# An LSTM cell in another order: a scan over pairs for the cell state, and the product of two transposed halves for the output

## The chip, the cores and the metric

One core of a Trainium2 chip. The metric is the device time of one execution in microseconds (us). Before the change: 1159.02 us, the median of three runs (1155.53 to 1159.16).

Engines are called as in the profile: PE (matrix engine; PEld is its weight load), DVE (vector), ACT (scalar), POOL (GpSimd), SP (it issues DMAs here). A name with a q at its end, such as DVEq, is the engine's sequencer.

## The reference

A graph network of two layers over 1250 nodes with 512 features, then an LSTM over the 1250 rows in order, both with a residual sum. The change touches the LSTM only. With x_t a row and h, c the state (512 values each):

```
f_t = sigmoid([x_t, h] W_f + b_f)      i_t = sigmoid([x_t, h] W_i + b_i)
g_t = tanh([x_t, h] W_c + b_c)         o_t = sigmoid([x_t, h] W_o + b_o)
c_t = f_t * c + i_t * g_t
h_t = o_t * tanh(c_t)
```

The output is x_t + h_t. All data are fp32.

## The kernel before, in words

The graph network and the part of the gates that depends on x alone (the products with the upper halves of the weights) take the first 557 us. Their sums are written to HBM (xp_d) as three bf16 planes for each row. The rest is the recurrence, in `lstm` (from line 759).

**Stretches.** The 1250 rows are cut into 32 stretches (P) of 40 rows (LEN), which run side by side. Each stretch starts from a zero state 90 rows early (WARM), so `lstm` runs 130 steps: 90 to warm up, 40 that give output. At the end the states at the ends of the stretches are compared with those that the next stretches had at their start (lines 813 to 824); only if they are apart would `in_order` run all rows one after the other. It did not run in the profiled execution.

**Layout.** On 128 partitions lie 4 blocks of 128 hidden values times 32 stretches. The state is cut once more along its free dimension into two halves s of 64 values. A tile of gates `p` is 128 x 4 x 64 in PSUM: forget, input, output, candidate.

**A step** (lines 796 to 808). `open_step` loads xs by SP and opens the gate sums with a small bf16 matmul (L532). `add_gates` (L540) adds h times the recurrent weights: 32 matmuls, which the profile counts as 64 instructions, since each has two in fp32. Their order is written by hand: 12 matmuls that need only half 0 of h, then 8 that close the gates of half 0 and need half 1 of h, then 12 more, which close the gates of half 1.

**The cell** (L547 to L558) runs once for each half: tanh of the candidate into the second half of tile cg, sigmoid of f and i, sigmoid of o; one product of (f, i) with (c, g), one sum into the first half of cg, tanh of it, the product with o, and a transpose in blocks of 32 x 32 on DVE into hT, which is what PE takes as weights in the next step.

**What sets the order.** The block stands under `tc.manual_schedule` for PE, DVE and ACT: these engines work through their instructions in the order of the program text, half 0's cell ahead of half 1's. Waits between engines, and of an engine for its own results, are put in by the framework as semaphores. hT has two buffers, the tiles of pool lstm_work (cells) three. In the 40 steps with output POOL adds hh to the residual x2c (L806), and after steps 8, 16, 24, 32, 38 and 40 the rows are stored by DMA.

Of the kernel before, what the change touches and what calls it, by code (L numbers as in the profile page):

```python
# [9 lines left out]
F32 = mybir.dt.float32  # L10
# [3 lines left out]
AF = mybir.ActivationFunctionType  # L14
OP = mybir.AluOpType
# [23 lines left out]
def gnn_lstm_kernel(  # L39
# [23 lines left out]
    nc = tc.nc  # L63
# [122 lines left out]
    with ExitStack() as gnn_stack:  # L186
# [14 lines left out]
        with tc.tile_pool(name="prep", bufs=1) as prep, \  # L201
# [20 lines left out]
            for name, v in (("fcb", fc_b), ("b1", b_1), ("b2", b_2)):  # L222
                b = prep.tile([R, D], F32, name=name)
# [317 lines left out]
                                     Wh[:, b, j, :, 64 * s:64 * (s + 1)],  # L541
                                     start=False, stop=(b == 3))

        def cell(pool, p, cg, s, hh, hT):

            m = slice(64 * s, 64 * (s + 1))
            nc.scalar.activation(cg[:, 1, :], p[:, 3, :], AF.Tanh)  # L547
            sg = pool.tile([128, 2, 64], F32, name=f"sg{s}")
            nc.scalar.activation(sg, p[:, 0:2, :], AF.Sigmoid)  # L549
            so = pool.tile([128, 64], F32, name=f"so{s}")  # L550
            nc.scalar.activation(so, p[:, 2, :], AF.Sigmoid)  # L551
            pr = pool.tile([128, 2, 64], F32, name=f"pr{s}")
            nc.vector.tensor_mul(pr, sg, cg)  # L553
            nc.vector.tensor_add(cg[:, 0, :], pr[:, 0, :], pr[:, 1, :])  # L554
            th = pool.tile([128, 64], F32, name=f"th{s}")
            nc.scalar.activation(th, cg[:, 0, :], AF.Tanh)  # L556
            nc.vector.tensor_mul(hh[:, m], so, th)  # L557
            nc.vector.transpose(hT.rearrange("p b c -> p (b c)"), hh[:, m])  # L558

        def in_order(pool, ps_g, Wh):  # L560

            cgs = [pool.tile([128, 2, 64], F32, name=f"cgs{s}") for s in range(2)]
            hT0 = [pool.tile([128, 2, 32], F32, name=f"hTs{s}") for s in range(2)]
            for s in range(2):
                nc.vector.memset(cgs[s], 0.0)
                nc.vector.memset(hT0[s], 0.0)
            with tc.For_i(0, N, 1) as t:
                xs = pool.tile([128, G], F32, name="xs")
                xr = pool.tile([128, 128], F32, name="xr")
                for j in range(4):  # L570
                    nc.sync.dma_start(
                        xs[32 * j:32 * (j + 1), :],
                        bass.AP(tensor=xw_d.tensor, offset=xw_d.offset + t * (4 * G) + j * G,
                                ap=[[0, 32], [1, G]]))
                    nc.sync.dma_start(
                        xr[32 * j:32 * (j + 1), :],
                        bass.AP(tensor=x2_d.tensor, offset=x2_d.offset + t * D + 128 * j,
                                ap=[[0, 32], [1, 128]]))
                x4 = xs.rearrange("p (g m) -> p g m", g=NG)
                ps = open_gates(ps_g, lambda j: ident[:, 32 * j:32 * (j + 1)],  # L580
                                lambda j, s: x4[:, :, 64 * s:64 * (s + 1)])
                add_gates(ps, hT0, Wh)
                hh = pool.tile([128, 128], F32, name="hhs")
                h1 = [pool.tile([128, 2, 32], F32, name=f"hT1{s}") for s in range(2)]
                for s in range(2):
                    cell(pool, ps[s], cgs[s], s, hh, h1[s])
                    nc.vector.tensor_copy(hT0[s], h1[s])
                nc.vector.tensor_add(xr, xr, hh)
                for j in range(4):
                    nc.sync.dma_start(  # L590
                        bass.AP(tensor=out.tensor, offset=out.offset + t * D + 128 * j,
                                ap=[[D, 1], [1, 128]]),
                        xr[32 * j:32 * j + 1, :])
# [165 lines left out]
        def lstm(late, Wh):  # L759

            TOL = 2.0 ** -18
            with tc.tile_pool(name="state", bufs=2) as state, \
                    tc.tile_pool(name="load", bufs=5) as load, \
                    tc.tile_pool(name="lstm_work", bufs=3) as cells, \
                    tc.tile_pool(name="seq", bufs=1) as seq, \
                    tc.tile_pool(name="ps_g", bufs=3, space=PSUM) as ps_g, \  # L770
                    tc.tile_pool(name="ps_c", bufs=1, space=PSUM) as ps_c:
                cgs = [seq.tile([128, 2, 64], F32, name=f"cg{s}") for s in range(2)]

                def keep_state(dst, hT):
                    for s in range(2):
                        nc.vector.tensor_copy(dst[:, 2 * s:2 * s + 2, :], hT[s])
                        nc.vector.transpose(
                            dst[:, 4 + 2 * s:6 + 2 * s, :].rearrange("p b c -> p (b c)"),
                            cgs[s][:, 0, :])

                x2c = base1.rearrange("b t (q m) -> b t q m", q=4)
                for j in range(4):
                    for i in range(T):
                        (nc.sync if i % 2 else nc.gpsimd).dma_start(
                            x2c[32 * j:32 * (j + 1), i, :, :], x2[:, i, 128 * j:128 * (j + 1)])
                x2c = x2c.rearrange("b i q m -> b (i q) m")
                snap = seq.tile([128, 8, 32], F32, name="snap")
                last = seq.tile([128, 8, 32], F32, name="last")
                stores = [8, 16, 24, 32, 38, LEN]
                with tc.manual_schedule(engines={mybir.EngineType.PE, mybir.EngineType.DVE,  # L790
                                                 mybir.EngineType.Activation}):
                    hT = [state.tile([128, 2, 32], F32, name=f"hT{s}") for s in range(2)]
                    for s in range(2):
                        nc.vector.memset(cgs[s], 0.0)
                        nc.vector.memset(hT[s], 0.0)
                    for n in range(-WARM, LEN):
                        if n == 0:
                            keep_state(snap, hT)
                        ps = open_step(load, ps_g, n)
                        add_gates(ps, hT, Wh)  # L800
                        hh = cells.tile([128, 128], F32, name="hh")
                        hT = [state.tile([128, 2, 32], F32, name=f"hT{s}") for s in range(2)]
                        for s in range(2):
                            cell(cells, ps[s], cgs[s], s, hh, hT[s])
                        if n >= 0:
                            nc.gpsimd.tensor_add(x2c[:, n, :], x2c[:, n, :], hh)  # L806
                            if n + 1 in stores:
                                store(x2c, ([0] + stores)[stores.index(n + 1)], n + 1)
                    keep_state(last, hT)

                apart = seq.tile([128, 8, 31], F32, name="apart")
                nc.vector.tensor_sub(apart, last[:, :, 0:31], snap[:, :, 1:32])
                nc.vector.scalar_tensor_tensor(apart, apart, -1.0, apart, op0=OP.mult, op1=OP.max)
                nc.vector.tensor_scalar(apart, apart, TOL, None, OP.is_le)
                near = seq.tile([128, 1], F32, name="near")
                nc.vector.tensor_reduce(near, apart.rearrange("p a b -> p (a b)"),
                                        mybir.AxisListType.X, OP.add)
                pc = ps_c.tile([1, 1], F32, name="pc")  # L820
                nc.tensor.matmul(pc, near, ones, start=True, stop=True)
                far = seq.tile([1, 1], I32, name="far")
                nc.vector.tensor_scalar(far, pc, -1.0, float(128 * 8 * 31), OP.mult, OP.add)
                n_far = nc.values_load(far, min_val=0, max_val=128 * 8 * 31)
                with tc.If(n_far > 0):
                    for i in range(T):
                        pl = pl_bufs[:, i % 2, :, :]
                        nc.sync.dma_start(pl.rearrange("b i g -> b (i g)"), tile_steps(i))
                        v = h.rearrange("b t d -> b (t d)")[:, :4 * G]
                        nc.vector.tensor_add(v, pl[:, 0, :], pl[:, 1, :])  # L830
                        nc.vector.tensor_add(v, v, pl[:, 2, :])
                        nc.sync.dma_start(in_time(xw_d, i), v)
                        nc.gpsimd.dma_start(in_time(x2_d, i), x2[:, i, :])
                    in_order(seq, ps_g, Wh)
# [57 lines left out]
```

## Time and profile before

| What | Value |
|---|---|
| Time of the profiled execution | 1157.69 us |
| Its span (first to last instruction) | 1155.9 us |
| Mean granted PE clock | 0.989 (1.00 from 557 to 1150 us) |
| Busy: PE, PEld, DVE, ACT, POOL | 1025.9, 535.2, 519.3, 344.4, 69.8 us |
| From 557 to 1150 us: PE, DVE, ACT, POOL busy | 511.3, 244.9, 202.7, 18.4 us |
| ACT: cg L547, sg L549, so L551, th L556, each x260 | 224, 271, 230, 256 ns |
| DVE: pr L553, cg L554, hh L557, hT L558, each x260 | 272, 225, 225, 246 ns |
| POOL: sum L806, x40 | 461 ns |

How to read it: a group of the page is a line of the source, an engine, the operation, its result and its sources, the shapes, how many there were, then the busy time in us and the mean of one in ns, and last the idle time of the engine just before them with what ended it. In the chain of waits, "issue" is time that no instruction fills. Matmuls are pipelined and their ends are modelled, so a busy PE is not a PE at its peak.

### The profile page before, as it was taken

The page shows a single profiled execution, that of the slowest core. Times are in us where ns is not written, and L with a number is a line of the kernel's source. Part 1 is how long each engine was busy: PE and PEld are TensorE (multiplying, and loading weights), DVE is VectorE, ACT ScalarE, POOL GpSimd, SP SyncE. Part 2 cuts the span into 40 slices and gives each one's busy share as a digit, 9 for nine tenths or more (in the row PEclk, how much of TensorE's full clock was granted, in tenths as well). Part 3 has the DMA queues.
Part 4 walks back from the last instruction along what each step waited for, and adds up shares of the span by engine and source line. Part 5 has one row for each costly group of instructions (what it writes and reads, how often), then busy time and mean ns, then how long its engine had stood idle before and what let it go on. Part 6 is the DMA issues. An engine that isn't in the chain of part 4 may idle for free.

```text
span 1155.9 us, 27516 instructions
## 1 busy us (share of the span) xinstructions
PE 1025.9 (89%) x11340; PEld 535.2 (46%) x11356; DVE 519.3 (45%) x1775; ACT 344.4 (30%) x1284; POOL 69.8 (6%) x123
## 2 busy tenths in 40 slices
PE   2999997799999999999788888888888888888886
PEld 1555544355455444444344444444444444444443
DVE  4956665401500665555444444444434444443444
ACT  2312212412500023333333333333333333333332
POOL 1000000300000281000000000000000000010011
PEclk9999999799999999999999999999999999999999
DMA  8000000800300175222632323232322333333331
GB/s 233 1 1 1 1 1 2 256 1 1 89 1 1 69 168 181 109 110 109 199 97 84 97 84 98 84 98 84 94 87 87 95 88 94 102 97 102 102 102 21
DMA packets 41466, 96.22 MB, mean 83 GB/s; under 512 B 6125, under 2 KB 21846, under 8 KB 39928
## 3 DMA queue, kind: packets, MB, share of 16 engines
q1 hardware_dynamic: 35012, 77.59, 22.3%
q0 software_dynamic: 4496, 14.09, 4.2%
q10 hardware_dynamic: 1819, 2.65, 0.8%
q8 instruction: 92, 1.51, 0.6%
q14 instruction: 47, 0.38, 0.1%
HBM read 71.93 MB, written 19.76 MB: 79 GB/s over the span
## 4 chain that ended last, share of the span: by engine, by line
PE 67%; DVE 16%; ACT 9%; issue 4%; DMA 3%; POOL 0%; DVEq 0%; ACTq 0%; SPq 0%
PE gates L540 28%; PE psM L166 15%; PE agg L685 11%; PE psM L510 10%; DVE pr L553 3%; ACT th L556 3%; DVE hT L558 3%; DVE hh L557 3%; DVE cg L554 3%; ACT cg L547 3%; PE acc L303 2%; ACT sg L549 2%; DMA base<-in_x_dram 2%; DMA bx<-in_L_ffn_b_i_dram 1%; PE psT L155 1%
## 5 line engine op out<-in xcount | busy, mean ns | idle before, releaser
L540 PE MATMUL gates<-Wh,hT 128*32 128x256 f32 x8320 | 482.5, 383 | 75.2 <-DVE hT L558 75.2
L540 PEld LDWEIGHTS gates<-Wh,hT 128*32 128x32 f32 x8320 | 244.7, 110 | 287.1 <-DVE hT L558 151.9
L553 DVE TENSOR_TENSOR pr<-sg,cg 128x128 f32<-128x128 f32 x260 | 70.6, 272 | 223.9 <-ACT sg L549 223.8
L685 PE MATMUL agg<-adj,planes 128*128 128x512 bf16 (+1 forms) x704 | 134.6, 352 | 10.0 <-ACT planes L415 7.2
L510 PE MATMUL psM<-Wx,xT 128*128 128x512 f32 x320 | 138.7, 594 | 1.5 <-ACT xT L160 1.5
L547 ACT ACTIVATE cg<-gates 128x64 f32<-128x64 f32 x260 | 58.2, 224 | 249.2 <-PE gates L540 245.6
L556 ACT ACTIVATE th<-cg 128x64 f32<-128x64 f32 x260 | 66.7, 256 | 138.6 <-DVE cg L554 138.6
L685 PEld LDWEIGHTS <-planes 128*128 128x128 bf16 x720 | 71.8, 100 | 73.0 <-ACT planes L415 7.6
L557 DVE TENSOR_TENSOR hh<-so,th 128x64 f32<-128x64 f32 x260 | 58.6, 225 | 86.4 <-ACT th L556 86.0
L510 PEld LDWEIGHTS psM<-Wx,xT 128*128 128x128 f32 x320 | 60.4, 190 | 76.8 <-issue 72.9
L558 DVE STREAM_TRANSPOSE hT<-hh 128x64 f32<-128x64 f32 x260 | 63.8, 246 | 27.9 <-DVE hh L557 0.9
L166 PE MATMUL psM<-w,hT 128*128 128x512 f32 x160 | 70.9, 596 | 0.0
L549 ACT ACTIVATE sg<-gates 128x128 f32<-128x128 f32 x260 | 70.5, 271 | 0.2
L554 DVE TENSOR_TENSOR cg<-pr 128x64 f32<-128x64 f32 x260 | 58.5, 225 | 8.9
L806 POOL TENSOR_TENSOR base<-base,hh 128x128 f32<-128x128 f32 x40 | 18.4, 461 | 693.0 <-issue 533.4
L551 ACT ACTIVATE so<-gates 128x64 f32<-128x64 f32 x260 | 59.8, 230 | 0.0
L532 PE MATMUL gates<-xs,sel 96*32 96x256 bf16 x1040 | 52.5, 272 | 4.2 <-DMA xs<-xp_d 4.2
L303 PE MATMUL acc<-od,ob 125*128 125x400 f16 (+22 forms) x360 | 47.9, 260 | 9.0 <-DVE od L289 8.2
L289 DVE TENSOR_SCALAR od<-ids,key 125x820 f16<-125x820 f16 (+42 forms) x160 | 55.6, 347 | 0.0
L287 DVE TENSOR_SCALAR ob<-ids,low 125x128 f16<-125x128 f16 x160 | 39.5, 247 | 16.3 <-PE acc L303 16.0
L166 PEld LDWEIGHTS psM<-w,hT 128*128 128x128 f32 x160 | 29.7, 190 | 34.0 <-issue 33.0
L303 PEld LDWEIGHTS <-ob 125*128 125x128 f16 x360 | 29.7, 98 | 31.6 <-issue 12.7
(154 smaller groups left out, 663.6 us busy)
## 6 DMA issues: line engine op xcount, KB each, us to landing
xs<-xp_d SPq DMA_DIRECT2D x130, 384.0 KB, 3.2
xp_d<-planes SPq DMA_DIRECT2D x10, 1536.0 KB, 5.4
w<-in_L_gnn_w_dram POOLq DMA_DIRECT2D x4, 1024.0 KB, 12.8
xp_d<-adj POOLq DMA_DIRECT2D x1, 1440.0 KB, 7.8
base<-x SPq DMA_DIRECT2D x20, 64.0 KB, 2.3
base<-x POOLq DMA_DIRECT2D x20, 64.0 KB, 2.6
fcw<-in_L_gnn_fc_w_dram POOLq DMA_DIRECT2D x1, 1024.0 KB, 8.6
out_dram<-base SPq DMA_DIRECT2D x12, 64.0 KB, 2.2
```

The source lines that it names most:

```text
L166: nc.tensor.matmul(p, lT[:, k, :], rhs[:, k, :], start=(k == 0), stop=(k == KD - 1))
L303: nc.tensor.matmul(blocks[i][:, (d0 - i * BW) * T:(d1 - i * BW) * T], ob, od[:, (d0 - lo) * T:(d1 - lo) * T], start=False, stop=last)
L510: nc.tensor.matmul(p, yT[:, k, :], Wx[:, k, j, :, :], start=(k == 0), stop=(k == KD - 1))
L540: nc.tensor.matmul(ps[s][32 * j:32 * (j + 1), :, :], hT[b // 2][:, b % 2, :], Wh[:, b, j, :, 64 * s:64 * (s + 1)], start=False, stop=(b == 3))
L547: nc.scalar.activation(cg[:, 1, :], p[:, 3, :], AF.Tanh)
L549: nc.scalar.activation(sg, p[:, 0:2, :], AF.Sigmoid)
L553: nc.vector.tensor_mul(pr, sg, cg)
L554: nc.vector.tensor_add(cg[:, 0, :], pr[:, 0, :], pr[:, 1, :])
L556: nc.scalar.activation(th, cg[:, 0, :], AF.Tanh)
L557: nc.vector.tensor_mul(hh[:, m], so, th)
L558: nc.vector.transpose(hT.rearrange("p b c -> p (b c)"), hh[:, m])
L685: nc.tensor.matmul(p[:, :n * R], planes[:, k, pl, f * 128:(f + 1) * 128], adj[:, k, t0:t0 + n, :].rearrange("b i r -> b (i r)"), start=(k ...
```

## The change

`cell` is replaced by a class `Half`, one object for each half, with tiles that live through all steps. `fi` is a tile of pairs (0, sigmoid value), `add` a tile of pairs (g, f*c), `c` the result of a scan over these pairs. Along the free dimension the scan computes state = data0 * state + data1. With data0 = (0, i) and data1 = (g, f*c) each pair yields first g and then i*g + f*c, which is the new cell state, at the second place of the pair. So there are 128 elements in the scan for 64 values of the state. Output gate and tanh of the cell are then transposed each by itself, and their product is written to hT at once. h without a transpose is no longer made on DVE: POOL computes it in the 40 steps with output.

```diff
-        def cell(pool, p, cg, s, hh, hT):
-
-            m = slice(64 * s, 64 * (s + 1))
-            nc.scalar.activation(cg[:, 1, :], p[:, 3, :], AF.Tanh)
-            sg = pool.tile([128, 2, 64], F32, name=f"sg{s}")
-            nc.scalar.activation(sg, p[:, 0:2, :], AF.Sigmoid)
-            so = pool.tile([128, 64], F32, name=f"so{s}")
-            nc.scalar.activation(so, p[:, 2, :], AF.Sigmoid)
-            pr = pool.tile([128, 2, 64], F32, name=f"pr{s}")
-            nc.vector.tensor_mul(pr, sg, cg)
-            nc.vector.tensor_add(cg[:, 0, :], pr[:, 0, :], pr[:, 1, :])
-            th = pool.tile([128, 64], F32, name=f"th{s}")
-            nc.scalar.activation(th, cg[:, 0, :], AF.Tanh)
-            nc.vector.tensor_mul(hh[:, m], so, th)
-            nc.vector.transpose(hT.rearrange("p b c -> p (b c)"), hh[:, m])
+        class Half:
+            def __init__(self, pool, s):
+                self.s = s
+                self.fi = [pool.tile([128, 2, 64, 2], F32, name=f"fi{s}{n}") for n in range(2)]
+                self.add = [pool.tile([128, 64, 2], F32, name=f"ad{s}{n}") for n in range(2)]
+                self.c = pool.tile([128, 64, 2], F32, name=f"c{s}")
+                self.n = 0
+                for t in self.fi:
+                    nc.vector.memset(t, 0.0)
+            def begin(self):
+                nc.vector.memset(self.c, 0.0)
+            def step(self, pool, p, so, tc, hT):
+                m = slice(64 * self.s, 64 * (self.s + 1))
+                fi, add = self.fi[self.n], self.add[self.n]
+                self.n = 1 - self.n
+                nc.scalar.activation(fi[:, :, :, 1], p[:, 0:2, :], AF.Sigmoid)
+                nc.scalar.activation(add[:, :, 0], p[:, 3, :], AF.Tanh)
+                nc.scalar.activation(so[:, m], p[:, 2, :], AF.Sigmoid)
+                nc.vector.tensor_mul(add[:, :, 1], fi[:, 0, :, 1], self.c[:, :, 1])
+                nc.vector.tensor_tensor_scan(
+                    *(t.rearrange("p m a -> p (m a)") for t in (self.c, fi[:, 1, :, :], add)),
+                    0.0, OP.mult, OP.add)
+                soT = pool.tile([128, 64], F32, name=f"soT{self.s}")
+                nc.vector.transpose(soT, so[:, m])
+                nc.scalar.activation(tc[:, m], self.c[:, :, 1], AF.Tanh)
+                tcT = pool.tile([128, 64], F32, name=f"tcT{self.s}")
+                nc.vector.transpose(tcT, tc[:, m])
+                nc.vector.tensor_mul(hT.rearrange("p b c -> p (b c)"), soT, tcT)
...
-                        hh = cells.tile([128, 128], F32, name="hh")
+                        so = cells.tile([128, 128], F32, name="so")
+                        th = cells.tile([128, 128], F32, name="th")
                         hT = [state.tile([128, 2, 32], F32, name=f"hT{s}") for s in range(2)]
                         for s in range(2):
-                            cell(cells, ps[s], cgs[s], s, hh, hT[s])
+                            halves[s].step(cells, ps[s], so, th, hT[s])
                         if n >= 0:
-                            nc.gpsimd.tensor_add(x2c[:, n, :], x2c[:, n, :], hh)
+                            nc.gpsimd.tensor_mul(th, so, th)
+                            nc.gpsimd.tensor_add(x2c[:, n, :], x2c[:, n, :], th)
```

`in_order` and `keep_state` are changed to the new names in the same way; the two clears of cg become clears of `c`, and four clears of the `fi` tiles come before the loop.

More of the change, by code (lines that the diff above doesn't have):

```diff
@@ L560, in in_order @@
         def in_order(pool, ps_g, Wh):
-            cgs = [pool.tile([128, 2, 64], F32, name=f"cgs{s}") for s in range(2)]
+            halves = [Half(pool, s) for s in range(2)]
             hT0 = [pool.tile([128, 2, 32], F32, name=f"hTs{s}") for s in range(2)]
             for s in range(2):
-                nc.vector.memset(cgs[s], 0.0)
+                halves[s].begin()
                 nc.vector.memset(hT0[s], 0.0)
@@ L582, in in_order @@
                 add_gates(ps, hT0, Wh)
-                hh = pool.tile([128, 128], F32, name="hhs")
-                h1 = [pool.tile([128, 2, 32], F32, name=f"hT1{s}") for s in range(2)]
+                so = pool.tile([128, 128], F32, name="sos")
+                th = pool.tile([128, 128], F32, name="ths")
                 for s in range(2):
-                    cell(pool, ps[s], cgs[s], s, hh, h1[s])
-                    nc.vector.tensor_copy(hT0[s], h1[s])
-                nc.vector.tensor_add(xr, xr, hh)
+                    h1 = pool.tile([128, 2, 32], F32, name=f"hT1{s}")
+                    halves[s].step(pool, ps[s], so, th, h1)
+                    nc.vector.tensor_copy(hT0[s], h1)
+                nc.vector.tensor_mul(so, so, th)
+                nc.vector.tensor_add(xr, xr, so)
                 for j in range(4):
@@ L771, in lstm @@
                     tc.tile_pool(name="ps_c", bufs=1, space=PSUM) as ps_c:
-                cgs = [seq.tile([128, 2, 64], F32, name=f"cg{s}") for s in range(2)]
+                halves = [Half(seq, s) for s in range(2)]
                 def keep_state(dst, hT):
@@ L778, in keep_state @@
                             dst[:, 4 + 2 * s:6 + 2 * s, :].rearrange("p b c -> p (b c)"),
-                            cgs[s][:, 0, :])
+                            halves[s].c[:, :, 1])
                 x2c = base1.rearrange("b t (q m) -> b t q m", q=4)
@@ L793, in lstm @@
                     for s in range(2):
-                        nc.vector.memset(cgs[s], 0.0)
+                        halves[s].begin()
                         nc.vector.memset(hT[s], 0.0)
```

## The prediction

> **What bounds the kernel now.** I read the page first: busy shares, the chain that ended last, the groups. PE is busy 89% of the span, yet the groups show that its recurrent matmuls wait for a transpose on the Vector engine.
>
> ```profile
> PE 67%; DVE 16%; ACT 9%; issue 4%; DMA 3%; POOL 0%; DVEq 0%; ACTq 0%; SPq 0%
> ...
> L540 PE MATMUL gates<-Wh,hT 128*32 128x256 f32 x8320 | 482.5, 383 | 75.2 <-DVE hT L558 75.2
> ```
>
> The LSTM fills the stretch from 557 to 1150 us, so 130 steps hold about half of the span, and the change lies in this half alone. So I next read the chain of waits over one step (start, duration, what).
>
> ```profile
> 803.02 0.22 ACT cg L547
> 803.25 0.18 ACT sg L549
> ...
> 803.45 0.30 DVE pr L553
> 803.75 0.02 issue
> 803.77 0.24 DVE cg L554
> ...
> 804.03 0.27 ACT th L556
> ...
> 804.32 0.24 DVE hh L557
> 804.56 0.03 issue
> 804.59 0.02 DVEq L558
> 804.61 0.04 issue
> 804.65 0.26 DVE hT L558
> ```
>
> This is half 0. Every piece is end to end: the next matmul starts at 804.96, 1.93 us after the first activation. Note the two kinds of gap on DVE. Between pr and cg it is 0.02; ahead of hT, which waits for hh on its own engine and for PE (which still reads the older hT buffer), a sequencer piece DVEq appears and the gap is 0.09. By the timeline's durations the gaps are 0.034 and 0.107. In the last 37 steps hh of half 0 waits for ACT and for POOL, and its gap grows from 0.03 to 0.10: a second engine to wait for costs 0.07 when the wait that comes last sits in the sequencer.
>
> Then I asked the timeline whether half 1 has slack.
>
> ```profile
> 804.65 0.25 DVE L558 STREAM_TRANSPOSE hT<-hh 128x64 f32<-128x64 f32 x1
> 804.82 0.25 DVE L553 TENSOR_TENSOR pr<-sg,cg 128x128 f32<-128x128 f32 x1
> 804.95 1.02 PEld L540 LDWEIGHTS gates<-Wh,hT 128*32 128x32 f32 x24 [0.83 <-DVE hT L558]
> 805.11 0.23 DVE L554 TENSOR_TENSOR cg<-pr 128x64 f32<-128x64 f32 x1
> 805.37 0.26 ACT L556 ACTIVATE th<-cg 128x64 f32<-128x64 f32 x1 [0.54 <-DVE cg L554]
> 805.99 0.24 DVE L558 STREAM_TRANSPOSE hT<-hh 128x64 f32<-128x64 f32 x1
> 806.28 1.89 PEld L540 LDWEIGHTS gates<-Wh,hT 128*32 128x32 f32 x40 [0.31 <-DVE hT L558]
> ```
>
> PE has 24 instructions that need only half 0. Sixty-four take 3.70 us with a tail of 0.40, so four start every 0.22 us and six fours last 1.32. Half 1's weights start 806.28 - 804.95 = 1.33 after half 0's. So half 1 is just in time, with no slack: its work on DVE begins only when half 0's hT is through. A step is therefore 1.33 (half 0's start to half 1's start) + 1.20 (16 more PE instructions, to the first activation) + 1.93 (half 0's cell) = 4.46 us. Both cells are on the path: a delay in half 0's counts, and a delay of half 1's behind it counts again.
>
> [...] No run here shows a scan yet. [...] 224 ns for 64 elements at L554, 291 (median of L553) for 128. [...] the set of sigmoid holds tanh too, and a load takes some 1283 ns. The trace agrees: 1.28 us, twice, and none after the first Sigmoid although Tanh follows 259 times. [...] I price the strided operands at nothing. No run here shows one[...].
>
> **The change, half 0.** Times count from the first activation. Old: pr at 0.42, cg ends at 0.98, th 1.01 to 1.27, hh from 1.30, hT ends at 1.88, PE at 1.93.
> - Sigmoid of f and i goes first (271 ns). The product f*c waits only for it: starts at 0.30, where pr starts at 0.42 (a gain of 0.12), and takes 0.224 for 64 elements, to 0.53. Tanh of the candidate starts 0.16 later than the sigmoid by ACT's spacing and ends by 0.39: covered by that product.
> - The scan needs the product (its own engine) and the candidate (ACT), of which DVE has not yet waited for the latter. That is a wait on two engines. In this trace the sequencer's separate wait was for DVE whenever an instruction waited for DVE and another engine (hT: DVE there, PE with the instruction), so the late wait sits there and the gap is 0.107; the other end is 0.034. I take 0.107. Start 0.63.
> - The scan itself: [...] I take 0.424: ends at 1.06, where cg ended at 0.98.
> - Tanh of the cell 1.09 to 1.35. The transpose of the output gate (0.246) lies on DVE meanwhile, done by 1.31 even if it starts 0.01 after the scan: hidden by tanh. If tanh did not cover it, 0.25 per half.
> - Transpose of tanh from 1.38 to 1.63, then the product. It writes hT, so the wait for PE moves from the transpose to it, with the same 0.107: 1.73 to 1.96, PE at 2.01. From tanh's end to PE is 0.66, as before: the two operations change places for nothing.
> Half 0 costs 2.01 - 1.93 = 0.08 a step.
>
> **Half 1.** DVE is in order: half 0's final product stands ahead. From the end of half 0's last DVE operation: the first product starts 0.08 early, as pr does, and ends at 0.11; scan 0.21 to 0.64 (cg ended at 0.43); tanh to 0.93; transpose 0.96 to 1.21; product 1.31 to 1.54; PE 0.05 later at 1.59, where it was 1.38. So PE waits 0.20 a step longer. The gain of 0.12 from the earlier sigmoid does not exist here, since the gates are ready long before DVE is.
>
> **Sum.** 0.08 + 0.20 = 0.285 us by unrounded terms; times 130 steps 37.0 us.
> - Table load: the load before L549 is on the chain (the first step takes 5.77 instead of 4.46). With Sigmoid first, its set is loaded while ACT waits for PE: -1.3 us.
> - Four clears of 128 x 256 (0.27 each, from 0.11 and 0.17 for 64 and 128): they lie before the first scan, while PE still waits for the first xs, and the first recurrent matmul waits only for the small clears, from 557.5 to 558.0, against its start at 561.3. Zero; without the cover 1.1 us.
> - hh's wait for POOL (0.07 in the last 37 steps) passes to tanh of the cell: no difference.
> - POOL gets a product beside the sum, 2 x 0.46 us in steps of 4.5: hidden. No DMA is issued or moved. After the last step POOL starts earlier by some 0.26 and works 0.5 longer, while DVE's comparison and the read of its result run to the end: zero.
> Against the profiled execution (1157.69, span 1155.9): 1157.69 + 37.0 - 1.3 = **1193.4 us**. That run lies 1.3 below the median shown, within its spread.
>
> **Rivals.**
> - **Faster**: the scan with the gap before it costs what the add it replaces does: 0.291 + 0.034 = 0.325. For it speaks that the old add sits 0.034 behind pr[...]. Then half 0 gains 0.123 and half 1 keeps its 1.33: -0.125 x 130 - 1.3, **1140 us**. The point that decides: gap and scan together below 0.39 make the kernel faster; I expect 0.531.
> - **Scan at one element a cycle, but behind the slow gap** (0.398 together): +0.02 a step, **1159 us**, no change.
> - **Half throughput, the gap the short one**: 0.146 a step less than forecast, **1174.5 us**.
> - **The product f*c waits for the candidate's tanh too**, because the two write alternate elements of one tile: it starts at 0.41, the scan then waits for one engine: 0.25 a step, **1189 us**.
> - **Three cycles an element, or strides that cost as much**: 0.133 in each half on top, **1228 us**.
>
> **How the numbers follow.** Chances: forecast 0.52, short gap 0.14, candidate waited for 0.08, three cycles 0.07 (all slower, 0.81); one element a cycle behind the slow gap 0.07 (same); faster 0.12. About 0.3%, 3.5 us, is what a measurement can tell from no change. The range reaches from the unchanged case up to the forecast with hundredths for the strides: 1157 to 1203 leaves out the faster case and the three cycles, 0.19.
>
> **What would show it.** In the changed profile: a scan group x260 of 0.42 us; a DVEq piece ahead of the scan and of the last product, none ahead of the transposes; the first product 0.30 after the sigmoid; half 1's 40 weight loads about 1.54 after half 0's 24, with idle time on PE waiting for half 1's hT; no table load inside the first step. A scan of 0.29 or a gap of 0.03 ahead of it makes the prediction wrong by the sizes above; so does a step shorter than 4.46 us.

## The result, and the profile after

The changed kernel takes 1211.7 us (median of six runs, 1210.2 to 1214.0), the kernel before 1159.4 beside it: ratio 1.046, interval 1.044 to 1.048. The profiled execution took 1210.81 us with a span of 1209.0. The forecast was 1193.4 with a range up to 1203: slower as expected, but by 52 us instead of 36.

The page's shares and groups after the change:

```profile
PE 50%; DVE 29%; ACT 11%; issue 6%; DMA 3%; DVEq 1%; ACTq 1%; POOL 0%
...
L540 PE MATMUL gates<-Wh,hT 128*32 128x256 f32 x8320 | 505.2, 383 | 106.7 <-DVE hT L578 100.5
...
L566 ACT ACTIVATE fi<-gates 128x128 f32<-128x128 f32 x260 | 74.3, 286 | 257.2 <-PE gates L540 257.1
...
L570 DVE TENSOR_TENSOR_SCAN c<-fi,ad 128x128 f32<-128x128 f32 x260 | 110.5, 425 | 27.2 <-DVE ad L569 0.5
...
L578 DVE TENSOR_TENSOR hT<-soT,tcT 128x64 f32<-128x64 f32 x260 | 69.6, 268 | 27.6 <-DVE tcT L577 0.9
```

DVE's share of the chain rose from 16 to 29%, PE's fell from 67 to 50%. The scan takes 425 ns, as priced (0.424 us). One row is odd: a product of 64 elements into hT takes 268 ns on the mean, where L554 and L557 took 225.

The chain of waits over half 0 of one warm-up step:

```profile
804.90 0.30 ACT fi L566
805.20 0.02 issue
805.22 0.24 DVE ad L569
805.46 0.03 issue
805.49 0.02 DVEq L570
805.51 0.04 issue
805.55 0.43 DVE c L570
805.99 0.02 issue
806.01 0.27 ACT th L575
...
806.30 0.26 DVE tcT L577
...
806.65 0.22 DVE hT L578
806.88 0.15 DVE ad L569
```

The chain goes from half 0's hT straight on into half 1's first product on DVE. Before, it went from hT to PE. The sequencer piece stands ahead of the scan, with a gap of 0.09. From the first activation to the end of hT it is 1.98 us. The timeline of the same step shows what PE gets:

```profile
806.79 0.22 DVE L569 TENSOR_TENSOR ad<-fi,c 128x64 f32<-128x64 f32 x1
806.93 1.02 PEld L540 LDWEIGHTS gates<-Wh,hT 128*32 128x32 f32 x24 [0.93 <-DVE hT L578]
807.12 0.42 DVE L570 TENSOR_TENSOR_SCAN c<-fi,ad 128x128 f32<-128x128 f32 x1
...
808.22 0.22 DVE L578 TENSOR_TENSOR hT<-soT,tcT 128x64 f32<-128x64 f32 x1
808.50 1.88 PEld L540 LDWEIGHTS gates<-Wh,hT 128*32 128x32 f32 x40 [0.55 <-DVE hT L578]
```

Half 1's weights start 1.57 us after half 0's (808.50 - 806.93), against 1.33 before, and PE's weight loads sit idle for the difference (0.55 us ahead of half 1's, 0.31 before). A warm-up step is 4.80 us (median; 4.46 before), close to the 4.745 forecast. But a step with output is 5.15, where it was 4.53 before: 0.27 more than the 0.34 that the warm-up steps lost. The timeline of one such step, at half 1's end:

```profile
1103.46 0.24 DVE L577 STREAM_TRANSPOSE tcT<-th 128x64 f32<-128x64 f32 x1 [0.20 <-ACT th L575]
1103.78 0.45 POOL L829 TENSOR_TENSOR th<-so,th 128x128 f32<-128x128 f32 x1 [4.16 <-DVE tcT L577]
1103.81 0.51 DVE L578 TENSOR_TENSOR hT<-soT,tcT 128x64 f32<-128x64 f32 x1
...
1104.37 1.88 PEld L540 LDWEIGHTS gates<-Wh,hT 128*32 128x32 f32 x40 [0.83 <-DVE hT L578]
```

The transpose of tanh (L577) releases two instructions at once: POOL's product of so and th, since DVE has now read th, and DVE's product into hT. POOL starts 0.03 us earlier. DVE then takes 0.51 us for what takes 0.225 elsewhere, and the weights of half 1 wait for it. In the timeline of the kernel before, POOL was beside DVE at the same place and cost nothing:

```profile
1144.74 0.46 POOL L806 TENSOR_TENSOR base<-base,hh 128x128 f32<-128x128 f32 x1 [4.09 <-DVE hh L557]
...
1144.76 0.25 DVE L558 STREAM_TRANSPOSE hT<-hh 128x64 f32<-128x64 f32 x1
```

There DVE's instruction has one source, here it has two. POOL starts first in both, by 0.02 and 0.03 us, and here DVE is the one that takes longer, 0.51 us. POOL's product, with 0.45, takes no longer than its sum (0.46 in both kernels). That it is the number of DVE's sources that matters, and not the kind of its instruction, no run here shows by itself.

**Theory.** Of the 53 us of span, 44 (0.342 x 130) come from the scan path: its rate, its wait on two engines, and half 1 queued behind half 0 on DVE. Another 11 (0.27 x 40) come from POOL's product against DVE's. **Rivals**: the output steps are longer for other reasons (ACT's waits for POOL's buffers, POOL's output that is later); or transposing apart costs in every step and the scan less than it seems.

### The profile page after: what moved, and what is told of

The parts are those of the page before. It is cut to its first block, busy times and chain, and to the rows that moved or that the text cites. A ratio compares the mean times of both kernels' runs of the same rounds, so it can differ in the third digit from the quotient of the medians.

```text
span 1209.0 us, 28078 instructions
## 1 busy us (share of the span) xinstructions
PE 1047.3 (87%) x11340; PEld 535.0 (44%) x11356; DVE 605.5 (50%) x2039; ACT 333.4 (28%) x1283; POOL 87.7 (7%) x163
## 4 chain that ended last, share of the span: by engine, by line
PE 50%; DVE 29%; ACT 11%; issue 6%; DMA 3%; DVEq 1%; ACTq 1%; POOL 0%
PE psM L166 14%; PE gates L540 12%; PE agg L707 10%; PE psM L510 9%; DVE c L570 9%; DVE hT L578 6%; ACT th L575 6%; DVE tcT L577 5%; DVE ad L569 4%; ACT fi L566 3%; PE acc L303 2%; DMA base<-in_x_dram 2%; PE psT L155 1%; DMA Wx<-in_L_ffn_W_i_dram 1%; DVE od L289 1%
## 5 line engine op out<-in xcount | busy, mean ns | idle before, releaser
L540 PE MATMUL gates<-Wh,hT 128*32 128x256 f32 x8320 | 505.2, 383 | 106.7 <-DVE hT L578 100.5
L569 DVE TENSOR_TENSOR ad<-fi,c 128x64 f32<-128x64 f32 x260 | 58.1, 223 | 209.8 <-ACT fi L566 209.8
L566 ACT ACTIVATE fi<-gates 128x128 f32<-128x128 f32 x260 | 74.3, 286 | 257.2 <-PE gates L540 257.1
L570 DVE TENSOR_TENSOR_SCAN c<-fi,ad 128x128 f32<-128x128 f32 x260 | 110.5, 425 | 27.2 <-DVE ad L569 0.5
L575 ACT ACTIVATE th<-c 128x64 f32<-128x64 f32 x260 | 68.1, 262 | 196.2 <-DVE c L570 196.2
L577 DVE STREAM_TRANSPOSE tcT<-th 128x64 f32<-128x64 f32 x260 | 63.8, 245 | 52.0 <-ACT th L575 51.6
L578 DVE TENSOR_TENSOR hT<-soT,tcT 128x64 f32<-128x64 f32 x260 | 69.6, 268 | 27.6 <-DVE tcT L577 0.9
L829 POOL TENSOR_TENSOR th<-so,th 128x128 f32<-128x128 f32 x40 | 18.2, 454 | 727.0 <-issue 564.9
L567 ACT ACTIVATE ad<-gates 128x64 f32<-128x64 f32 x260 | 58.2, 224 | 0.0
L574 DVE STREAM_TRANSPOSE soT<-so 128x64 f32<-128x64 f32 x260 | 57.2, 220 | 0.0
```

Of the source, the lines that this page charges most:

```text
L540: nc.tensor.matmul(ps[s][32 * j:32 * (j + 1), :, :], hT[b // 2][:, b % 2, :], Wh[:, b, j, :, 64 * s:64 * (s + 1)], start=False, stop=(b == 3))
L566: nc.scalar.activation(fi[:, :, :, 1], p[:, 0:2, :], AF.Sigmoid)
L569: nc.vector.tensor_mul(add[:, :, 1], fi[:, 0, :, 1], self.c[:, :, 1])
L570: nc.vector.tensor_tensor_scan(*(t.rearrange("p m a -> p (m a)") for t in (self.c, fi[:, 1, :, :], add)), 0.0, OP.mult, OP.add)
L575: nc.scalar.activation(tc[:, m], self.c[:, :, 1], AF.Tanh)
L577: nc.vector.transpose(tcT, tc[:, m])
```

## The experiments

Eleven kernels, each timed in four runs beside seven of the kernel before (1158.0 to 1158.2 in each group).

**The product on DVE.**

```diff
-                            nc.gpsimd.tensor_mul(th, so, th)
+                            nc.vector.tensor_mul(th, so, th)
```

> The kernel after, with h = so*tanh(c) in the 40 output steps computed by DVE (one 128x128 product behind half 1's hT, while PE works) instead of by POOL; POOL keeps the sum. Theory (POOL's product starts together with DVE's last product and the two block each other): hT of half 1 falls from about 0.51 back to 0.23 us in these steps, the output steps go from 5.15 to about 4.87 us, 40 x 0.28 = 11 us less than the kernel after: about 1200.5. Rival (the output steps are longer because of ACT's extra waits for POOL's buffers, or because POOL's output is later): hT stays long or the steps stay at 5.1, 1210 to 1212.

Measured: 1200.6 us (ratio 1.038, 1.036 to 1.039), 11.1 below the changed kernel. The group of hT in the stretch from 1030 to 1140 us, which holds output steps alone:

```profile
L578 DVE TENSOR_TENSOR hT<-soT,tcT 128x64 f32<-128x64 f32 x45 | 10.1, 225 | 4.7
```

A step with output is 4.86 us. The work moved to DVE (284 ns a step) is free, since DVE is idle there: 1.38 us are left ahead of the next step's first product. The rival of buffers and late output falls: ACT still waits for POOL's buffers in these steps, and POOL still gives its sum later than half 1's hT.

**The scan alone**, with the output as before (one product, one transpose, POOL only adds).

```diff
-                soT = pool.tile([128, 64], F32, name=f"soT{self.s}")
-                nc.vector.transpose(soT, so[:, m])
-                nc.scalar.activation(tc[:, m], self.c[:, :, 1], AF.Tanh)
-                tcT = pool.tile([128, 64], F32, name=f"tcT{self.s}")
-                nc.vector.transpose(tcT, tc[:, m])
-                nc.vector.tensor_mul(hT.rearrange("p b c -> p (b c)"), soT, tcT)
+                th = pool.tile([128, 64], F32, name=f"th{self.s}")
+                nc.scalar.activation(th, self.c[:, :, 1], AF.Tanh)
+                nc.vector.tensor_mul(tc[:, m], so[:, m], th)
+                nc.vector.transpose(hT.rearrange("p b c -> p (b c)"), tc[:, m])
```

> The scan with its order of activations, but the output as before: one product o*tanh(c) on DVE, one transpose into hT; POOL only adds. Theory (the scan, its gap and the slower strided sigmoid make the warm-up steps longer; transposing apart is neutral there): warm-up step about 4.80 us as in the kernel after, output steps 0.07 more, total about 1200. Rival (transposing apart with its extra transpose costs part of it): warm-up step clearly below 4.80, total near 1180.

Measured: 1200.2 us (1.036 to 1.039), a warm-up step of 4.78 and an output step of 4.85. The scan carries nearly all of the warm-up steps' loss, 0.32 of 0.34 us. In the output steps POOL's sum lies beside the transpose into hT again, and the transpose takes its usual 0.245.

**Transposing apart alone**, with the cell state as before (pr and cg).

```diff
...
+            soT = pool.tile([128, 64], F32, name=f"soT{k}")
+            nc.vector.transpose(soT, so[:, m])
-            nc.scalar.activation(th, cg[:, 0, :], AF.Tanh)
-            nc.vector.tensor_mul(hh[:, m], so, th)
-            nc.vector.transpose(hT.rearrange("p b c -> p (b c)"), hh[:, m])
+            nc.scalar.activation(th[:, m], cg[:, 0, :], AF.Tanh)
+            thT = pool.tile([128, 64], F32, name=f"thT{k}")
+            nc.vector.transpose(thT, th[:, m])
+            nc.vector.tensor_mul(hT.rearrange("p b c -> p (b c)"), soT, thT)
...
-                            nc.gpsimd.tensor_add(x2c[:, n, :], x2c[:, n, :], hh)
+                            nc.gpsimd.tensor_mul(th, so, th)
+                            nc.gpsimd.tensor_add(x2c[:, n, :], x2c[:, n, :], th)
```

> The cell state as before (one product, one sum), but output gate and tanh transposed apart, their product into hT, and h made by POOL. Theory: warm-up step unchanged at 4.46 us; in the output steps POOL's product blocks DVE's last one by about 0.28 us, 40 x 0.28 = 11 us: about 1170. Rival (POOL's product is harmless, and transposing apart costs in every step): 1159 if both are neutral; if apart costs, a warm-up step above 4.50.

Measured: 1170.9 us (ratio 1.011, 1.009 to 1.013). The collision is there without any scan; the group of hT from 1030 to 1140 us:

```profile
L559 DVE TENSOR_TENSOR hT<-soT,thT 128x64 f32<-128x64 f32 x45 | 16.5, 366 | 4.7
```

(366 is the mean of half 0's 0.22 and half 1's 0.51.) But the warm-up step is 4.48, not 4.46: transposing apart does cost 0.025 a step. The trace shows where. The instruction that opens half 1 on DVE, pr, takes 0.250 in the kernel before, where it follows a transpose, and 0.284 here, where it follows a product:

```profile
803.79 0.23 DVE L559 TENSOR_TENSOR hT<-soT,thT 128x64 f32<-128x64 f32 x1
803.93 0.28 DVE L552 TENSOR_TENSOR pr<-sg,cg 128x128 f32<-128x128 f32 x1
```

Why it takes longer stays open. What stands ahead of it is not the only thing that counts, as "The same in the kernel before" will show.

**Tanh of the candidate first.**

```diff
+                nc.scalar.activation(add[:, :, 0], p[:, 3, :], AF.Tanh)
                 nc.scalar.activation(fi[:, :, :, 1], p[:, 0:2, :], AF.Sigmoid)
-                nc.scalar.activation(add[:, :, 0], p[:, 3, :], AF.Tanh)
```

> The kernel after with the candidate's tanh issued ahead of the sigmoid of f and i. Then DVE's product waits for a later activation, and the scan waits for DVE alone. Theory (the gap of 0.107 ahead of the scan is the price of waiting for two engines): half 0 starts 0.12 later and gains 0.07, half 1 gains 0.07; the step is 0.02 to 0.03 shorter, and the first step has its table load back (+1.3): about 1209 to 1211, with a gap of 0.034 ahead of the scan. Rival (the gap belongs to the scan): the gap stays, half 0 loses 0.12 a step, 16 us: about 1228.

Measured: 1209.2 us (ratio 1.046, 1.043 to 1.048). The chain of waits there:

```profile
800.16 0.24 DVE ad L569
800.40 0.02 issue
800.43 0.43 DVE c L570
```

No sequencer piece, a gap of 0.02. The gap ahead of the scan thus belongs to its second wait, not to the scan, and the order that was to gain 0.12 by an early product gains nothing overall.

**A shorter scan**: the first 32 pairs of each half. Half of the cell state is left out.

```diff
-                    *(t.rearrange("p m a -> p (m a)") for t in (self.c, fi[:, 1, :, :], add)),
+                    *(t.rearrange("p m a -> p (m a)")[:, :64]
+                      for t in (self.c, fi[:, 1, :, :], add)),
```

> The kernel after with the scan over the first 32 pairs of each half only (64 elements); the other half of the cell state stays zero, so this leaves out half of the recurrence of c. Theory [...]: the scan takes 0.291 instead of 0.425 us, both halves count, 2 x 0.134 x 130 = 35 us less: about 1177. Rival (one cycle an element with a longer fixed part): 0.358, 17 us less: about 1194.

Measured: 1179.6 us (ratio 1.019, 1.016 to 1.022), 32 below the changed kernel. The page's group:

```profile
L570 DVE TENSOR_TENSOR_SCAN c<-fi,ad 128x64 f32<-128x64 f32 x260 | 76.0, 292 | 27.2 <-DVE ad L569 0.5
```

425 - 292 = 133 ns for 64 elements: 2.08 ns each, twice the 1.03 of a plain product ((291 - 225) / 64, from pr and cg before). The one cycle an element of the rivals stands for that rate of a product; with it the shorter scan would have taken 0.36. The step fell from 4.80 to 4.54, by both halves' 0.133.

**POOL writes only**: a clear in place of POOL's product; h is left out of the output.

```diff
-                            nc.gpsimd.tensor_mul(th, so, th)
+                            nc.gpsimd.memset(th, 0.0)
```

> The kernel after with POOL's product in the output steps replaced by a clear of the same tile at the same place (it waits for the same transpose and starts at the same time); h is left out of the output. Theory [...]: a POOL instruction that only writes does not block DVE's last product, hT of half 1 back to 0.23 us, about 1200.5 as with the product on DVE. Rival (any POOL instruction at that time, or its writes, slows DVE): 1206 to 1212.

Measured: 1199.7 us (1.033 to 1.038); the group of hT from 1030 to 1140 us:

```profile
L578 DVE TENSOR_TENSOR hT<-soT,tcT 128x64 f32<-128x64 f32 x45 | 10.1, 225 | 4.7
```

POOL's clear (205 ns) starts beside DVE's product as before, and the product takes its usual time:

```profile
1106.35 0.20 POOL L829 MEMSET th<- 128x128 f32 x1 [4.11 <-DVE tcT L577]
1106.39 0.23 DVE L578 TENSOR_TENSOR hT<-soT,tcT 128x64 f32<-128x64 f32 x1
```

This says less than was expected of it, since the clear is so short. Under a hold until 0.08 us after POOL's end, as in the next run and in the changed kernel, the product would take 0.24 us (205 - 44 + 79 ns, with the 44 ns by which POOL starts ahead). It takes 0.226. So the profile speaks against a hold by POOL's writes with 15 ns only, and the time of the run does not tell.

**POOL reads one source**: `nc.gpsimd.tensor_copy(th, so)` at the same place.

> The kernel after with POOL's product replaced by a copy of so into th (one source); tanh is left out of the output, not of the recurrence. Theory (a POOL instruction that reads SBUF blocks a DVE product with two sources): hT of half 1 is longer than 0.23 us in the output steps by up to what the copy takes, 1203 to 1212. Rival (only a POOL instruction with two sources does): about 1200.5.

Measured: 1202.1 us (1.036 to 1.041), just under the range expected and, by time alone, not clear of 1200.6. The timeline decides:

```profile
1103.59 0.29 POOL L829 COPY th<-so 128x128 f32<-128x128 f32 x1 [4.13 <-DVE tcT L577]
1103.63 0.33 DVE L578 TENSOR_TENSOR hT<-soT,tcT 128x64 f32<-128x64 f32 x1
```

DVE's product is held up by 0.10 us. It ends 0.08 us after POOL's copy (median of 40), as it ends 0.08 after POOL's product in the changed kernel. So a POOL instruction that reads one source is enough, and of the two measured the longer one holds DVE's product for longer: 0.29 us on POOL for 0.33 on DVE, 0.45 for 0.51.

**DVE's wait for PE taken early, in the kernel of the first experiment.**

```diff
                         for s in range(2):
+                            nc.vector.memset(hT[s][:, 0, 0:1], 0.0)
+                        for s in range(2):
                             halves[s].step(cells, ps[s], so, th, hT[s])
```

> The kernel of e1 (after, with h computed by DVE in the output steps) and, while DVE is idle ahead of half 0, a clear of one column of each new hT: this takes DVE's wait for PE, so that the last product waits for DVE alone. Theory (a wait on two engines costs 0.07 more where the late one sits in the sequencer): the gap ahead of the last product falls from 0.107 to 0.034 in both halves, 2 x 0.073 x 130 = 19 us less than e1: about 1181.5. Rival (the gap is the price of the dependence on a transpose): no change, 1200.5, or a little above for the clears.

Measured: 1181.9 us (ratio 1.020, 1.016 to 1.024), 18.7 below the first experiment. The gap ahead of the last product falls from 0.104 to 0.034 us in both halves (medians). The second wait costs 0.07 for this product as for the scan.

**The same in the kernel before.** This and the next two build a version that beats both.

> The kernel before with the same clear of one column of each new hT ahead of half 0's first product, so that the transpose into hT waits for DVE alone. Theory: the gap falls from 0.107 to 0.034 in both halves; half 0 gains 0.073 a step, but half 1 only 0.01, because PE needs 1.32 us for the 24 instructions of half 0 and was kept waiting only 0.01: 0.084 x 130 = 11 us less: about 1148. Rival (the gap belongs to the transpose): 1158 to 1160. If half 1 counted in full: 1139.

Measured: 1141.9 us (ratio 0.986, 0.983 to 0.989), 16 below the kernel before where 11 were expected. The step falls from 4.46 to 4.35. Half 0's cell gives 0.07 of it, and from half 0's weights to the next step's first activation it is 2.50 us instead of 2.53, where a gain of 0.01 was expected. PE's limit is as I had read it: half 1's weights now start 1.29 after half 0's, but the 25th matmul starts 1.32 after the first (1.33 before). The rest, 0.02, lies between that matmul and the activation, and I have no reason for it. The chain of waits:

```profile
801.32 0.02 issue
801.34 0.02 ACTq L547
801.36 0.04 issue
801.40 0.22 ACT cg L547
...
802.70 0.24 DVE hh L557
802.94 0.02 issue
802.96 0.26 DVE hT L558
```

No DVEq ahead of hT any more: the second wait costs a transpose 0.07, too. One sequencer piece is left, ahead of the first activation. And pr of half 1, which follows a transpose here as in the kernel before, takes longer:

```profile
802.82 0.27 ACT L549 ACTIVATE sg<-gates 128x128 f32<-128x128 f32 x1
...
802.96 0.25 DVE L558 STREAM_TRANSPOSE hT<-hh 128x64 f32<-128x64 f32 x1
...
803.13 0.28 DVE L553 TENSOR_TENSOR pr<-sg,cg 128x128 f32<-128x128 f32 x1
```

It takes 0.281 in the warm-up steps, where ACT's sigmoid ends 0.04 ahead of its start, and 0.250 in the output steps, where the sigmoid ends 0.11 ahead, as in the kernel before. So the longer time goes with a product ahead of it in one kernel and with a late result of ACT in the other.

**The wait for POOL taken early too, and the sigmoid first.**

```diff
-            nc.scalar.activation(cg[:, 1, :], p[:, 3, :], AF.Tanh)
             sg = pool.tile([128, 2, 64], F32, name=f"sg{s}")
             nc.scalar.activation(sg, p[:, 0:2, :], AF.Sigmoid)
+            nc.scalar.activation(cg[:, 1, :], p[:, 3, :], AF.Tanh)
...
                         for s in range(2):
+                            nc.vector.memset(hT[s][:, 0, 0:1], 0.0)
+                            nc.vector.memset(hh[:, 64 * s:64 * s + 1], 0.0)
+                        for s in range(2):
                             cell(cells, ps[s], cgs[s], s, hh, hT[s])
```

> As e6, and in the same way a clear of one column of each half of hh, which takes the wait for POOL, and the sigmoid of f and i ahead of the candidate's tanh (one table load less). Theory: 0.07 less in the last 37 steps (2.6 us), 1.3 for the table load, about 0.01 a step for the order (1.2): about 5 us below e6, 1143. Rival (only the wait for PE mattered): as e6.

Measured: **1131.3 us** (ratio 0.976, 0.973 to 0.979), the fastest of the study together with the next one, and 10.6 below the kernel ahead of it, where 5 were expected. Its chain at the same place:

```profile
802.18 0.02 issue
802.21 0.28 ACT sg L548
```

The piece on ACT is gone as well, which I had not foreseen. The tanh into cg, a tile that lives through all steps, was first and waited for PE and for ACT's own earlier results; the sigmoid into a fresh buffer of sg waits for PE alone. From PE to the first activation it is 0.02 instead of 0.08, and the step is 4.29, in all steps alike.

**ACT's own wait taken early.** Two buffers for cg, and a copy of one column of tanh(c) by ACT at a step's end.

> As e9, with two buffers for cg and a copy of one column of tanh(c) by ACT at the end of a step, which takes ACT's wait for its own results, so that the first sigmoid waits for PE alone. Theory: the sequencer piece ahead of the first activation goes and half 0 starts some 0.06 earlier, 8 us: about 1135. Rival (the time from PE to ACT stays, since the wait for PE is the late one either way): 1143.

Measured: 1131.7 us (0.975 to 0.981), the same as the one before: the wait that it was to remove was gone already.

## Why the prediction was right and wrong

- **The bound and the two halves: right.** The sum of a step by half 0's cell and half 1's delay held. Half 0 costs 0.10 (forecast 0.08), half 1 0.24 (forecast 0.20), 0.342 in all against 0.285.
- **The scan: right**, 0.425 us against 0.424, half the rate of a product (shorter scan), and so was the wait on two engines that I put ahead of it (tanh first). The half rate was my estimate: no run ahead of the forecast showed a scan. With it the times of the products before give the forecast's figure: 0.291 for 128 elements and 0.067 for every 64 more (0.291 - 0.224), 0.291 + 2 x 0.067 = 0.425 for twice as many. The strides, which I had put at nothing without a run that showed one, cost DVE's first product as little as that: 0.227 in half 0, against 0.225 for the sum without strides before.
- **Output gate's transpose, table load, clears, tail: right.** None of the first three is in the chain, and from the last hT to the end it is 6.48 us, where it was 6.36. No table load is left inside the first step: the one load of the LSTM, 1.28 us, starts at 557.62 while ACT waits for PE, and the first activation at 564.09.
- **The step that failed**: "POOL gets a product beside the sum, 2 x 0.46 us in steps of 4.5: hidden." I asked only whether POOL had time. POOL is off the path, but DVE's last product is not: POOL's product starts with it and holds it for 0.28 us (0.509 against 0.225), in 40 steps, 11 us (the first experiment: 11.1). The same swap that I costed at nothing, "the two operations change places for nothing", put an instruction with two sources where one with a single source had stood, beside POOL. This carries the time out of the range: without it the changed kernel takes 1200.6 (the first experiment), inside the range.
- **Two terms mis-sized**, 7 us together. Half 1's first product was to take 0.18, on the pattern of pr behind a transpose; behind a product it takes 0.22 (it is 0.183 in the kernel with the scan alone, where it follows a transpose). And the sigmoid takes 0.29 instead of 0.27. The kernel that runs it first without a stride has 0.277, so of the 0.02 some 0.006 goes with being first and 0.015 is left. Writing every second element may be the reason, but that is not shown: half 1's sigmoid, with the same stride, takes 0.286 in the warm-up steps and 0.267 in the output steps. (0.342 - 0.285) x 130 = 7.4.
- With the 11 us and the forecast's 36 that makes 54, some 1 to 2 more than measured; in single steps of both kernels, before and after, there are delays of 0.1 to 0.4 us that I have not assigned.

## What to carry to other kernels

An engine off the critical path can still cost: for each instruction that moves to POOL, ask which DVE instruction the same event releases, and look at the two side by side in a trace. Here POOL's product beside DVE's product of two sources cost 0.28 us, and POOL's sum beside DVE's transpose nothing (0.245, as without POOL). Count the engines that a critical instruction waits for: a second one cost 0.06 to 0.07 us in each place tried here, and on DVE a clear of one column while the engine is idle took it off. Where two halves go through one engine in order and both are on the path, as here, the price of an operation counts twice (the shorter scan took 0.13 off each).

## What was not expected of the hardware

The scan's 0.425 us was foreseen (0.424); these were not. DVE's product with two sources ended 0.08 us after POOL's reading instruction, whether that took 0.29 or 0.45 us. Beside a POOL clear of 0.205 it took its usual 0.225. The same product of 128 elements took 0.250 on DVE behind a transpose and 0.284 behind another product, and behind a transpose 0.281 again where ACT's result came only 0.04 ahead of it. ACT's first activation came 0.02 after PE's result where it waited for PE alone, and 0.08 after it where it waited for an earlier result of its own as well.
